# Softmax sums over pairs of tiles: half of a layer's exponentials are added in twos on VectorE before TensorE sums them, and every engine's order is written anew

## The chip, the cores and the metric

One core of a Trainium2 chip runs the whole program. The metric is the device time of one execution in microseconds. Three executions of the kernel before took 3888.88, 3893.77 and 3896.64 us; their median, 3893.77 us, is the time before. Another execution was recorded by the hardware profiler; its rows are the source of all durations below.

## What is computed

The reference is one transformer layer on 16 images of 512 x 512 pixels:

```
h = patches(x) @ W + b                      # 1024 tokens of 256 per image
q, k, v = split(layernorm(h) @ w_qkv)       # 8 heads of 32
k = sum over f of a_f*sin(f*k) + b_f*cos(f*k), f = 1..256   # elementwise
h = h + softmax(q @ k.T * 32**-0.5) @ v @ w_out + b_out
h = h + shared_mlp(layernorm(h)) + top-2 of 4 experts
```

For the change only the softmax matters. The kernel never subtracts a maximum. It forms E = exp(scale * scores) with the keys on the partitions, and then two products with E as the moving operand: E with the values, and E with a block of ones. The second gives the sum of the exponentials of each query, already spread over the 32 rows that the division needs.

## The kernel before

**Tiling.** An image has four pairs of heads, and a pair has two halves of its queries, so there are 16 * 4 * 2 = 128 attention steps (`att`). A step walks over eight tiles of 128 keys (`kc`). For each `kc`:

- `score` (L1233): two matmuls (token S) write a tile of 128 keys x 1024 columns (two heads of 512 queries) into PSUM. The tile is one of two buffers, `big0` and `big1`, of two banks each.
- `exponential` (L1249): one ScalarE activation (token F) reads that tile and writes `es`, a 128 x 1024 tile in SBUF, one of five.
- `weigh` (L1261): token W, two groups of four matmuls. Each group uses the TensorE array as four column tiles of 32 and adds to one half of the PSUM tile `av`: the first with 32 columns of `v` as weights, the second with `ones32`. fp32 matmuls are issued in two passes, so the profile counts eight instructions for a group.

After the eighth tile, `normalize` (L1288) takes the reciprocal of the sums and multiplies, on VectorE.

**The other work in the same stretch.** The key transform of the following heads runs beside the attention. GpSimd turns integer phases (`turn_waves`, token T), ScalarE takes sines (`sine`, token F), TensorE mixes them into a PSUM tile (`mix`, token M, the array as 64 x 32 tiles), VectorE multiplies (`times_fast`, token P), and TensorE sums (`add_up`, token R). The mix tiles use the same two buffers `big0` and `big1` as the scores, in strict turns: each fill of a big tile must wait for the reader of the fill two places before. Four chains of further work (digits 0 to 3: keys, queries, values, tokens, projection and networks) use two PSUM banks of their own, `side0` and `side1`.

**Who sets the order.** Nothing is ordered at run time. `ORDERS` (L76) holds, for each of the five engines, a string in which each character is the next piece of work on that engine. `run` (L552) reads the strings and records the instructions; each engine then executes its own in that order, waiting only for data and buffers. VectorE's characters are P (`prod`), K (`keys`), N (`norm`), D (`spread`, a shuffle of 128 x 1024) and the chains' digits. `lay` (L527) records for each big tile who reads it last; `USERS` (L65) names that reader, `prod` for M and `exp` for S. The next fill of the buffer depends on it.

A digit's work on TensorE can be issued in two forms: with the whole 128 x 128 array (L408), or as four column tiles of 32 (L411). `tiling_of` (L384) takes the form that fits the neighbours, because a change of the array's form costs TensorE time.

**Values.** `values` (L740) projects two tiles of 128 tokens into a side bank; ScalarE copies them into `v` and, for the last pair of heads, into `last`, from where GpSimd copies them later (`last_values`, L768).

Of the kernel before, what the change touches and what calls it, by code (L numbers as in the profile page):

```python
# [11 lines left out]
FP = mybir.dt.float32  # L12
# [6 lines left out]
P = 128  # L19
# [29 lines left out]
NES = 5  # L49
GS = 4  # L50
# [20 lines left out]
    DVE: {"P": "prod", "K": "keys", "N": "norm", "D": "spread"},  # L71
# [7 lines left out]
        "33333331311",  # L79
        "111111000000FFFFFFFFFFF0FF0F0FF0FFF3333F33FFFFFFFFFFFF3",  # L80
        "333311113333000011130000000003D0D30PD0PD03PDPDDD3333PP00330D",
        "1100100T0TTTTTTTTTTTTTTTT0",
        "XXXXXXXX10XWWAA0AAWWWWW00WWW00W0WWWWXWAWAXWXAWQWAXQWX",
# [3 lines left out]
        "00300300303",  # L87
        "3333F3FFFFFFFFFFFFFFFFFFFF",
        "P3DP33333DK",
        "T3TTT3TTTTT0TTTT3TTT3TTTT0TTTTT0TTTTTT0T",  # L90
        "0WWXSWWKWWKWWWXWA0WQA0AWWAWXWXWWW",
# [3 lines left out]
        "MM00RM00M0R0MM3R3033M3M3RM3M30R3MM3SSRS0SSWWSSWS30WMMWWWWMMRSSRSSWWSSWSSW3WWWMW0MMMRSSRS"  # L95
        "SWSWSSWSWWWW0WMMMRM0SSRSSWSWSSWSWWWMWMW0MRMSSSWSWSSWSSWRWWWWMMMMRSSSWSSWSWSSWWRWWW0M0MM0"
        "M0SSRWSSRWWSS3WS3SWWWW3MM31RMM1SSRSWSSWSWSSWWWWW3MM31MRSS0SMWWWS3SR3SS1SWWWWW0MMMRMS0SSR"
        "WSS1W1SS1W1S0WWWW1MMW1RM1S01SMWSS1SSW1SSWRW101WMMWWWR1MM1SSR1SSW1SSWWSS1W1MMWWWWMMRS0S1S"
        "R1SSW1W1SS1SWWW01WMMW1RWMM3SS1SS1SSWWW1SSWRWWWW301MM131SS0S1SSRWMMWWS0SSR310WMMWWWWR1SM1"
        "SMWW3SS1SSW3SSRWWWW1MMW3RMM1SS0SS1SSWWRSSW1WW3MMWWW3M13SSR1SSWMW1WS3SW31SSWR1WWW1MM01R1M"  # L100
        "M1SS0SSRWWSSW1SSW01WW1WMMW0RMM10SS1SSRW1WSSW1SSW1WW1MMWWSS3SS0SSRWWMMW1SSW0RWWW1MM1W3R1M"
        "M1SS3S1SSWWWSS1SRWW1WWW101",
        "FFFFFFFFFFFFFFFFFFFFFFFFFFFFFFFFFFFFFFFFFFFFFFFFFFFFFFFFFFFFFFFFFFFFFFFFFFFFFFFFFFFFFFFF"
        "FFFFFFFFFFFFFFFF0FFF0FFF0FF0FFFF3333F3F3FFFFFFFFFFFFFFFFFFFFFFFFFFFFFFFFFFFFFFF3333F3F3F"
        "FFFFFFFFFFFFFFFF11F1F1F1F1F1F2FFFFFF1FFF1FFFF1F2F1FFF1FF1FFF1FFFFFF1FFFFFF1FF1FFFFFFFFFF"
        "FFFFFFFF1111FFF1F1FF1FF21FFFFFF1FFFFF1FFF2FF1FF1FFF1FFFFFFFF10FFFF1FFFF0FFF1F0FFFFFFFF10"
        "FFFFFFF3F3F33F3FFF3FFFFFFFFFFFFFFFFFFFFFFFFFFFFF111FFF1FFF1FFFFF13333F31F32FFFF1FFFF1FFF"
        "1FFF1F21FFFFFF1FFF1FFFFFFF1FFFFFFF1FF1FFFFFFFFFFFFFFFFFFFFF1F11F1FFFF1FF1FFF1FFFFFF12FFF"
        "1FFFF1F2FF1FFFF1F",
        "PPD0003PPDD3DD000030PP0NPPNNDNDDDKNNPPPPNNDDDD030NPPNNNPPDDKD0DPNPNPNPND0DDDNNNPNPPPDDKD"  # L110
        "NDPPNNPPN3333DDDDN3NPNNP1PPDDK1D3N3NDPNNP331P333D0PD00DD11111N0P0P0PNPDNN000DDK1002PPD0N"
        "PDNN2NP0D2DDPPN1NPPNDND10KD1D11111PPPPNNDNND0D1D2PP0NNPP2NND2DK3DN3NNDPP31NDPPDDD3P3P333"
        "1NNPNN1PDD1DKDPP1NNNPP3D1ND10DD0111110P3PNNN3NP33333DPD1DKD2NPP0N0N0PP2D2N00D0DD000PPNN0"
        "PP1NND0DK1D1D1PPNN1111N3NDPP0DD0DPPN3N1NPPN2DDK32D2NNNDN",
        "TTTTTTTTTTTTTTTTTTTTTTTTTTTTTTTTTTTTTTTTTTTTTTTTTTTTTTTTTTTTT3TTTT3TTTTTTTTTTTTTTT0TTTTT"
        "3TTTTTT0TTT1T0TT3TT0TTTTTTTT022T2TT2TTTTTTTTTTTTTTTTTTTTT1TTTTTTTTTTTTT2222TTTTTTTTTTTTT"
        "TTTTTTTTTTT3TTTTT3TTTTTTT0TTTTTTT1TTTT0TT3TTT3TTTTTTTT2022T2TTT0TTTT0TTTTTTTTTTTTTTTT1TT"
        "TTTTTTTTTT2TTTTTT22T2TTT",
        "S0WKWWKWWQWWAWW0AXAWWA0WWWWSWWKQWW0WKWW0WWQWAAWAAWWWQWWWSWQKWWWKWWWAQAWWWXAAWWWWSWWXKWWW"
        "WWWKWWQAAW0AWAWWWQXW0XWWSW0KWKW0WWWQW0WAWAAAWWWWWWW0SWQKKWWWW10QWWWAWAXWA0WWAWWQWWSWKWKX"  # L120
        "WWWXQXWWWWQAWWAWWAAWW1WWSWKWXKWWWWWWAQXXQWAWWAAXWW0WWXWSWWKWKWW0WWQAWAA0W0WAWW0WWQW0WSK1"
        "WKWXWWWWW0QW0AAWWWWAAQXXWWWQWSKK",
    ),
    (
        11,
        "MM1MMR1RSS10SS1SSW1WW1SSW0WWWWMM1RMM3SS0SSWWRSS1SS3WWWWWW1MM310MM1SSRRSS1SSWWSSW3W3WMMWW"
        "3W31SSR1SSW1MMW1S3SWR3SSWW10W1WMMW1RMM1S0S1SSWWR1SS0SSWW1WWWW10MM10MM1SSRWSS1WWR1SS0SS1W"
        "WWWWMM1SSR0WSSWMMWW1SS31SSWRWWW13MM13MMR1SS1SSWWSS1SSWRW1WWWW101",
        "F1FFF1FF10FFFF1F1F0FFFFFF0FFFFFFFFFFF0FFFF3333F3FFFFFFFF3FFFFFFFFFFFFFFFFFFF1F1F1FF1FFFF"
        "1FF1FF331332F3F3FF2FF1FFFFF1FFFF1FFF1FF1FFF1FFF1FFFFF1FFFFFFFF1FF1FFFFFFFFFFFFFFFFFFFFFF"  # L130
        "1111F1F1FFFFF1FFFFFFFFFF12FFF1FFF12FFF1FFFFF1F",
        "PPPP1DDDD1NNPP1PNPND3D3333KDD1N1PNNPN10PP010D1DD11131DP3P3NN3N333N3DPP1D2DKD000P2PN2NPPN"
        "N0D00DD0D00NN0P1PNPPND0D1DKD10NPNNP1N111D1D0PP3DDNNNN3P1PP3PD22DD2KNNDNN",
        "TTTTTTTTTTTTTTTTT3TTTTTT0TTT3T0TTTTT1TTTTTTT3TTTT22TTTTT20TT2T3T0TTTTT0TTTTTTTTTTTTTTTTT"
        "T1TTTTTTTTTTTTTT22T2TTTT2TT",
# [39 lines left out]
def plain_path(ctx: ExitStack, tc: tile.TileContext, a: dict, out: bass.AP, verdict: bass.AP):  # L175
# [1073 lines left out]
    def exponential(att, kc):  # L1249
# [7 lines left out]
        if old >= 0:  # L1257
            deps.append(("av", *divmod(old, NT)))
# [887 lines left out]
```

## Time and profile before

| what | value | where |
|---|---|---|
| median of three runs | 3893.77 us | times |
| profiled execution's own time | 3891.19 us | times |
| its span, first to last instruction | 3889.6 us | page |
| TensorE (PE) busy | 3789.0 us, 97% | page, part 1 |
| ScalarE (ACT) busy | 3261.8 us, 84% | page, part 1 |
| GpSimd (POOL) busy | 3199.8 us, 82% | page, part 1 |
| VectorE (DVE) busy | 2530.3 us, 65% | page, part 1 |
| DMA engines, largest queue | 81.5% of 16 engines' span | page, part 3 |
| granted TensorE clock | 0.992 of full | times |

In the page, part 1 gives the busy time of each engine and its share of the span. Part 2 cuts the span in 40 slices of 97 us; a digit is the busy share in tenths. Part 5 has groups of equal instructions: line, engine, operation, output and inputs, sizes, count, then total busy time, mean duration in ns of one, and the engine's idle time just before them. Busy time of TensorE overlaps, since a matmul starts before the one in front has drained: four column tiles start 7 ns apart, and what they cost the engine is read from one group's start to the next one's, not from the mean.

### The profile page before, as it was taken

How to read it: one execution, taken by the hardware profiler on the slowest of the kernel's cores; microseconds unless marked ns; L12 is line 12 of the kernel's file. 1: busy time of each engine (PE TensorE's matmuls, PEld its weight loads, DVE VectorE, ACT ScalarE, POOL GpSimd, SP SyncE). 2: the span in 40 equal slices, each digit the busy share in tenths (PEclk: the TensorE clock that was granted, in tenths of full speed). 3: DMA queues.
4: the chain of work that ended last, by engine and by line, in shares of the span. 5: the costliest groups of instructions: out<-in, count | busy, mean ns of one | idle time of the engine just before them, and what ended most of it. 6: DMA issues, size and time to landing. Idle time of an engine off the chain costs nothing.

```text
span 3889.6 us, 104231 instructions
## 1 busy us (share of the span) xinstructions
PE 3789.0 (97%) x41057; PEld 1937.2 (50%) x41057; DVE 2530.3 (65%) x4075; ACT 3261.8 (84%) x3939; POOL 3199.8 (82%) x2328
## 2 busy tenths in 40 slices
PE   6899999999999999999999999999999999999998
PEld 4434454454545555455454545555455454544444
DVE  3756757667675766757667676766767667676652
ACT  1799888888888988888888888888888888888983
POOL 3989878788888888888888888888888888888860
PEclk8999999999999999999999999999999999999999
DMA  6998878879879888888979889788888889878760
GB/s 210 265 270 236 259 228 236 256 215 275 232 242 249 225 268 233 254 234 241 253 219 274 229 246 255 218 269 236 251 243 240 252 225 277 221 232 246 224 173 18
DMA packets 589668, 916.61 MB, mean 236 GB/s; under 512 B 60876, under 2 KB 179572, under 8 KB 589172
## 3 DMA queue, kind: packets, MB, share of 16 engines
q1 hardware_dynamic: 588036, 909.40, 81.5%
q8 instruction: 327, 5.36, 0.6%
q14 instruction: 169, 1.38, 0.1%
q10 hardware_dynamic: 1136, 0.47, 0.1%
HBM read 758.64 MB, written 150.99 MB: 234 GB/s over the span
## 4 chain that ended last, share of the span: by engine, by line
PE 79%; DMA 7%; ACT 6%; DVE 3%; issue 2%; POOL 2%; SPq 1%; ACTq 0%; POOLq 0%; DVEq 0%
PE av L1271 20%; PE sT L1238 11%; PE kan L1139 10%; PE red L1172 5%; DMA w<-ud 4%; PE tok L411 4%; PE tok L408 4%; PE e3p L408 3%; PE e1p L408 3%; PE e1p L411 2%; ACT w L1119 2%; PE proj L408 2%; PE k L408 2%; PE s1p L411 2%; PE lnT L417 1%
## 5 line engine op out<-in xcount | busy, mean ns | idle before, releaser
L1109 POOL TENSOR_TENSOR w<-w,lane 128x1024 int32<-128x1024 int32 x1024 | 1928.2, 1898 | 296.4 <-DMA w<-ud 186.4
L1253 ACT ACTIVATE es<-sT 128x1024 f32<-128x1024 f32 x1024 | 1014.1, 1024 | 339.2 <-PE sT L1238 309.2
L1109 POOL TENSOR_TENSOR f<-f,lane 128x1024 int32<-128x1024 int32 x512 | 972.0, 1898 | 152.0 <-DVE f L1094 89.5
L1119 ACT ACTIVATE w<-w 128x1024 f32<-128x1024 int32 x1024 | 1016.1, 1048 | 58.8 <-POOL w L1109 47.7
L1153 DVE TENSOR_TENSOR f<-kan,f 128x1024 f32<-128x1024 f32 x512 | 613.3, 1218 | 291.5 <-PE kan L1139 135.3
L1238 PE MATMUL sT<-q,k 128*128 128x512 f32 x2048 | 677.2, 446 | 21.4 <-ACT es L1253 7.4
L1094 DVE STREAM_SHUFFLE f<-src 128x1024 int32<-128x1024 int32 x512 | 686.4, 1369 | 0.7
L1271 PE MATMUL av<-es,v 128*32 128x256 f32 x8192 | 638.9, 384 | 5.9 <-ACT es L1253 5.5
L1271 PE MATMUL av<-es,ones 128*32 128x256 f32 x8192 | 630.0, 379 | 0.0
L1139 PE MATMUL kan<-w,coef 64*32 64x512 f32 x8192 | 525.3, 597 | 8.3 <-ACT w L1119 6.9
L1119 ACT ACTIVATE f<-f 128x1024 f32<-128x1024 int32 x512 | 514.9, 1046 | 4.6 <-POOL f L1109 4.6
L1238 PEld LDWEIGHTS sT<-q,k 128*128 128x128 f32 x2048 | 359.0, 189 | 258.0 <-issue 104.5
L1271 PEld LDWEIGHTS av<-es,v 128*32 128x32 f32 x8192 | 228.4, 109 | 348.9 <-issue 225.4
L1295 DVE RECIPROCAL rc<-av 128x256 f32<-128x256 f32 x128 | 224.6, 1755 | 265.1 <-PE av L1271 264.9
L1271 PEld LDWEIGHTS av<-es,ones 128*32 128x32 f32 x8192 | 266.4, 110 | 176.1 <-issue 0.5
L1139 PEld LDWEIGHTS kan<-w,coef 64*32 64x32 f32 x8192 | 129.9, 105 | 295.9 <-issue 129.3
L1172 PE MATMUL red<-f,pack 128*32 128x512 f32 x2048 | 272.7, 602 | 3.2 <-DVE f L1153 3.1
L411 PE MATMUL tok<-wt,x 128*32 128x256 f32 x3456 | 199.8, 379 | 3.2 <-DVE h L643 3.2
L1119 ACT ACT_TABLE_LOAD x128 | 164.2, 1283 | 21.9 <-DMA w<-ud 19.7
L408 PE MATMUL tok<-wt,x 128*128 128x256 f32 x672 | 161.4, 393 | 14.9 <-DMA x<-in_xT 11.2
L1391 ACT ACT_TABLE_LOAD x128 | 164.2, 1283 | 2.2
L605 ACT ACTIVATE hn<-h,less,rstd 128x256 f32<-128x256 f32 x256 | 138.2, 595 | 21.6 <-POOL less L597 21.1
(150 smaller groups left out, 4257.1 us busy)
## 6 DMA issues: line engine op xcount, KB each, us to landing
w<-ud SPq DMA_DIRECT2D x2048, 256.0 KB
q<-qd SPq DMA_DIRECT2D x512, 128.0 KB
k<-kd SPq DMA_DIRECT2D x256, 256.0 KB
x<-in_xT SPq DMA_DIRECT2D x128, 384.0 KB
ud<-u SPq DMA_DIRECT2D x64, 512.0 KB
ud<-ui SPq DMA_DIRECT2D x64, 512.0 KB
src<-ud SPq DMA_DIRECT2D x512, 64.0 KB
qd<-qhi SPq DMA_DIRECT2D x64, 256.0 KB
```

Source lines behind the costliest of these rows:

```text
L408: nc.tensor.matmul(out=out, lhsT=lhsT, rhs=rhs, start=start, stop=stop)
L411: nc.tensor.matmul(out=out[ts(i, 32)], lhsT=lhsT[:, ts(i, 32)], rhs=rhs, start=start, stop=stop)
L1094: nc.vector.stream_shuffle(w, sources[g // 8].rearrange("p r n -> p (r n)"), [4 * (g % 8) + i // 8 for i in range(32)],)
L1109: nc.gpsimd.tensor_tensor(w, w, f.to_broadcast([P, N]), ALU.mult)
L1119: nc.scalar.activation(x, w, AF.Sin, scale=TURN * 2.0**-32)
L1139: nc.tensor.matmul(out=ps[ds(64 * j + 32 * blk, 32), ts(r, 512)], lhsT=coef[ts(r, 64)].rearrange("p e f j -> p (e f j)"), rhs=w[ts(r, 64), ...
L1153: nc.vector.tensor_mul(w, kan.pop(g), w)
L1172: nc.tensor.matmul(out=rows_of_pair[p][ts(2 * i + r, 32), :], lhsT=pack[:, ds(PACK0 - 16 * (k % 2) - 2 * (k // 2), 32)], rhs=prod[:, ts(r, ...
L1238: nc.tensor.matmul(out=ps[:, ts(s, 512)], lhsT=k4[kc // 4][:, s, ts(kc % 4, P)], rhs=q4[:, s, :], start=True, stop=True,)
L1253: nc.scalar.activation(es, scores.pop(kc), AF.Exp, scale=SCALE)
L1271: nc.tensor.matmul(out=acc[0][ts(i, HD), ts(half, 256)], lhsT=ones32 if half else v[:, kc, p % NPAIR, ts(i % 2, HD)], rhs=es[:, ds(512 * ( ...
L1295: nc.vector.reciprocal(rc[0], acc[0][:, 256:512])
```

## The change

In each attention step the key tiles 1 and 5 are put in `SUMMED`. Such a tile and the one in front of it form a pair, so two of the four pairs of a step, (0,1) and (4,5), are treated in a new way; (2,3) and (6,7) stay as they were.

- The first tile of a pair goes through `exponential` as before, but is multiplied with the values only, not with the ones.
- The second tile's exponentials are written back into its own score tile in PSUM. A new VectorE operation, `pair_sum` (token U), adds them to the first tile's and writes the sum into SBUF. The sum is multiplied with the values and with the ones.
- So that the result stays the same, the values of the first tile are stored as a difference: E0*V0 + E1*V1 = E0*(V0 - V1) + (E0 + E1)*V1. `values` forms V0 - V1 on VectorE out of the side bank, after ScalarE has copied V1.
- The big buffer of a summed tile is freed by `pair_sum`, no longer by the exponential. The SBUF tile of the pair's first tile is freed by its own matmuls and by the sum.
- The five order strings are replaced throughout.

The core of the diff, with the order strings left out:

```diff
+SUMMED = (1, 5)
...
-    DVE: {"P": "prod", "K": "keys", "N": "norm", "D": "spread"},
+    DVE: {"U": "sum", "P": "prod", "K": "keys", "N": "norm", "D": "spread"},
...
-            user = USERS.get(kind)
+            user = "sum" if kind == "S" and key[2] in SUMMED else USERS.get(kind)
...
-            yield ACT, 0.56
-            src = ps.rearrange("p t (i s d) -> p t i s d", s=2, d=HD)
-            for s in range(2):
-                nc.scalar.copy(
-                    v[:, ds(t0, 2), 0 : NPAIR - 1, ds(HD * s, HD)],
-                    src[:, :, 0 : NPAIR - 1, s, :],
-                )
-            nc.scalar.copy(last[:, ds(t0, 2), :, :], src[:, :, NPAIR - 1, :, :])
+            held = chains[now["chain"]]["bank"]
+            yield ACT, 0.31
+            chains[now["chain"]]["bank"] = held
+            homes = (
+                (v[:, :, 0 : NPAIR - 1, :].rearrange("p t i d -> p t (i d)"), slice(0, 192)),
+                (last, slice(192, 256)),
+            )
+            if t0 + 1 not in SUMMED:
+                for home, part in homes:
+                    nc.scalar.copy(home[:, ds(t0, 2), :], ps[:, :, part])
+                continue
+            for home, part in homes:
+                nc.scalar.copy(home[:, t0 + 1, :], ps[:, 1, part])
+            yield DVE, 0.42
+            for home, part in homes:
+                nc.vector.tensor_sub(home[:, t0, :], ps[:, 0, part], home[:, t0 + 1, :])
...
-            es = exps[kc] = esp.tile([P, 1024], FP, tag=f"es{(att * NT + kc) % NES}", name="es")
-            nc.scalar.activation(es, scores.pop(kc), AF.Exp, scale=SCALE)
...
+            ps = es = scores[kc]
+            if kc not in SUMMED:
+                es = exps[kc] = esp.tile([P, 1024], FP, tag=f"es{(att * NT + kc) % NES}", name="es")
+            nc.scalar.activation(es, ps, AF.Exp, scale=SCALE)
...
+    def tile_free(att, kc):
         old = att * NT + kc - NES
+        if old < 0:
+            return []
+        deps = [("av", *divmod(old, NT))]
+        return [*deps, ("sum", old // NT, old % NT + 1)] if old % NT + 1 in SUMMED else deps
+
+    def pair_sum(att, kc):
+        def action():
+            both = exps[kc] = esp.tile([P, 1024], FP, tag=f"es{(att * NT + kc) % NES}", name="both")
+            nc.vector.tensor_add(both, scores[kc], exps[kc - 1])
+
+        deps = [("exp", att, kc - 1), ("exp", att, kc)] + tile_free(att, kc)
+        put(DVE, "sum", 1.14, deps, ("sum", att, kc), action)
...
-            for half in range(2):
+            for half in range(1 if kc + 1 in SUMMED else 2):
...
-        deps = [("exp", att, kc)]
+        deps = [("sum" if kc in SUMMED else "exp", att, kc)]
...
-        put(PE, "W", 0.86, deps, ("av", att, kc), action)
+        put(PE, "W", 0.43 if kc + 1 in SUMMED else 0.86, deps, ("av", att, kc), action)
```

`last_values` makes one copy in place of two.

## The prediction

> **What bounds the kernel now.** First the totals and the slices.
>
> ```profile
> PE 3789.0 (97%) x41057; PEld 1937.2 (50%) x41057; DVE 2530.3 (65%) x4075; ACT 3261.8 (84%) x3939; POOL 3199.8 (82%) x2328
> ...
> PE   6899999999999999999999999999999999999998
> ```
>
> TensorE has no slice under nine tenths but the first two and the last. The busy times by stage (columns: stretch, its length, busy time of PE, weight loads, DVE, ACT, POOL, then clock, DMA share, GB/s) say how tight that is:
>
> ```profile
> 0.00:30.00 30.00, 18.78 (x80) 16.32 (x81) 4.90 (x17) 3.23 (x5) 4.07 (x26) 1.00 0.74 207
> ...
> 100.00:150.00 50.00, 37.72 (x348) 17.14 (x348) 34.63 (x54) 33.60 (x50) 45.61 (x34) 0.87 0.94 259
> ...
> 200.00:300.00 100.00, 92.01 (x1029) 35.55 (x1020) 60.42 (x82) 90.71 (x97) 89.88 (x49) 0.98 0.96 262
> ...
> 1000.00:2000.00 1000.00, 992.40 (x11068) 517.40 (x11057) 669.19 (x1072) 870.18 (x1058) 852.06 (x611) 1.00 0.86 243
> 2000.00:3000.00 1000.00, 994.60 (x11169) 514.98 (x11168) 681.55 (x1107) 873.11 (x1057) 857.97 (x626) 1.00 0.85 243
> ```
>
> From 400 us on TensorE idles 5 to 8 us in a thousand; ACT, POOL and DMA stand at 85 to 87%. In the first 300 us DMA (up to 0.96) sets the pace. So a TensorE microsecond is a microsecond of the kernel over some 95% of the attention, until waits appear. They hardly exist now (engine, line waited for: total us, times, longest):
>
> ```profile
> PE sT L1238 <- ACT es L1253: 7.4, 13, 1.9
> ...
> PE sT L1238 <- DVE f L1153: 5.2, 10, 1.0
> ```
>
> These two, with kan<-DVE f 0.9 and kan<-ACT es 0.2, are the waits for a big PSUM buffer: 13.7 us in all. It is the resource that the change strains.
>
> **What is removed.** Counted in both instruction orders, the matmuls with ones go from 4096 to 3072, so 256 groups of four are gone: 128 steps x 2 pairs. The change does what it says. A group's cost is read from starts in the timeline, since busy times overlap (start, busy us):
>
> ```profile
> 1904.33 0.61 PE L1271 MATMUL av<-es,ones 128*32 128x256 f32 x8
> 1904.76 0.61 PE L1271 MATMUL av<-es,v 128*32 128x256 f32 x8
> 1905.19 0.61 PE L1271 MATMUL av<-es,ones 128*32 128x256 f32 x8
> ```
>
> The starts are 0.43 us apart: 256 x 0.43 = **110 us** off TensorE. (Part 5's 630.0 us over 1024 groups would give 0.615 us and 157 us; it counts each drain.)
>
> **What the new order adds on TensorE.** Each change of the array's form costs. I took the time from the first matmul of one group to the first of the next, less streaming, median per kind of change, and counted the changes before and after (for whole to 128x32, whose median 0.28 holds waits for scores, I take 0.235, the lower quartile):
>
> - whole to 128x32: 389 to 478, at 0.235: +20.9 us
> - 128x32 to whole: 308 to 428, at 0.144: +17.3
> - 64x32 to 128x32: 135 to 189, at 0.171: +9.2
> - 128x32 to 64x32: 215 to 238, at 0.138: +3.2
> - whole to 64x32: 69 to 96, at 0.104: +2.8
> - 64x32 to whole: 149 to 145, at 0.171: -0.7
>
> Together 309 more changes, **+53 us** (46 to 57 with the least and the median value of the first kind). The Trainium skill (TensorEngine Tiling, Tiling Modes) says that changing the mode, not just the tile, drains the engine: a rule against this change, which halves the gain by cutting the stream finer. It states no price. TensorE: Matmul & The Clock Gate (What happens when you issue a matmul) puts a drain at about 128 cycles, at 2.4 GHz 53 ns; as an estimate that makes 309 x 0.053 = 16 us and a net gain of 94. The rows show two to four times that, and I go by them: net 110 - 53 = 57 us, of which 95%, **54 us**, falls where TensorE is the bound.
>
> **What VectorE gets.** The 256 sums read PSUM and SBUF and write SBUF, as the product does:
>
> ```profile
> L1253 ACT ACTIVATE es<-sT 128x1024 f32<-128x1024 f32 x1024 | 1014.1, 1024 | 339.2 <-PE sT L1238 309.2
> ...
> L1153 DVE TENSOR_TENSOR f<-kan,f 128x1024 f32<-128x1024 f32 x512 | 613.3, 1218 | 291.5 <-PE kan L1139 135.3
> ```
>
> 256 x 1.22 = 312 us, and 32 differences of 192 and of 64 columns at about 0.35 and 0.22 us (scaled from the 256-column addition, 0.42, and the 512-column one, 0.69) are 18: busy 2860 us, 75% of the new span. That much hides beside TensorE; what doesn't is its latency.
>
> **What ScalarE gets.** 256 exponentials write PSUM in place of SBUF, a form that the trace doesn't have. ScalarE: Activation LUTs (Step-by-step) calls PSUM the faster port for its output. The nearest row is the same activation into SBUF, 1.024 us. VectorE: DVE Perf Modes (The TRN2 errata) has the other side, reading PSUM rather than SBUF, at 52 cycles of 1.2 GHz less, 0.043 us; carried over to the write, as an estimate, it makes 0.98. The widest row of its size is the sine, 1.048. I take 1.02; from -11 to +6 us on an engine that isn't the bound, under 0.05 us on each sum's path. The value copies get cheaper (64 x (2 x 0.32 + 0.29) = 60 us to some 43, by row lengths). Both hide under TensorE's 97%; without that cover they'd be worth -17 us. The side bank is held longer for 32 of 64 value tiles, by ScalarE's wake-up and 0.6 us of VectorE. GpSimd's 16 copies for 32 save nothing that waits. No DMA is added; the queue orders are other permutations of the same transfers.
>
> **The wait that is added.** A big buffer with a summed tile is held by score, exponential and sum, and the fill two places on, score or mix, waits, with everything behind it in TensorE's single queue. In the trace the exponential ends at the soonest 1.24 us after the scores have streamed (median 1.6), the product 1.55 after the mix; the next fill follows within 0.05. A summed tile thus needs 1.24 + 0.06 + 1.22 + 0.05 = 2.57 us at least. Against that I set the streamed TensorE work, with the changes' prices, between a big tile and the next fill of its buffer, and carried each shortfall forward:
>
> - before, at these least delays: 11 short fills, 5 us, nearly all before 400 us. The measured 13.7 us answers to delays about 0.4 us longer.
> - after: of 256 summed tiles a quarter have under 2.94 us of cover (median 3.37) and 39 fall short; so do 28 after plain exponentials and 19 after products. After 400 us the shortfall is 13 us at the least delays, 33 with 0.3 us more, 42 with 0.4, 76 with 0.6.
>
> More work is packed between scores, but less than the hold grows. 138 of the 256 sums stand right behind a spread (1.37 us) and 43 behind the step that closes a normalization, so VectorE will often be some tenths late: I take **+30 us**, between 13 and 76. Behind a late sum waits its W as well, but it has 3.65 us of cover in nine of ten cases.
>
> **The sum.** Span 3889.6 - 54 + 30 = 3865.6. The median of the runs lies 4.2 us above that span (2.6 above the profiled execution's own 3891.19): 3870. The first 300 us are ordered anew as well and may give or take some 10 us; ScalarE's relief shortens exponential waits a little, for which I take 4 off. Predicted: **3866 us**, -0.7%.
>
> **Rivals.**
>
> *The sums hide* (chance 0.15): the order meets VectorE in time, the wait stays near 13 us or the start gains. 3894 - 54 + 8 to 13 = about 3848. For it: VectorE has 1360 us idle. Against: 39 sums lack cover even at the least delay.
>
> *The big buffers become the bound* (0.26, slower): in place, the PSUM buffers of summed tiles. If sums come 0.6 us over the least delay, the shortfall is 76 us against 54 gained: 3894 + 22 = 3916. It decides from about 0.48 us of mean lateness, where the shortfall reaches 54. For it: a spread or reciprocal (1.75 us) in front of a sum costs more than that if it starts late, and VectorE goes from 65 to 75%. Against: before, exponentials came 0.36 late in the median and cost 13.7 us.
>
> *Another engine is the bound already* (0.09, no change): the wave transfers hold GpSimd (186.4 us of its waits are on them), DMA is at 0.85, and the chain that ended last has 7% DMA. Then the freed time turns into TensorE idle and the median is about 3892. Against: ACT, POOL and DMA each have 13% to spare, and 1.4% is asked.
>
> **How the numbers follow.** The forecast as told has 0.50; with the hidden sums 0.65 faster by over 0.2%. 0.2%, 8 us, is about what a measurement of this kernel tells from no change. No change: 0.09. Slower: 0.26. The range leaves out the best half of the first rival and the worst of the second: 3838 to 3916; the forecast's own is 3848 to 3885.
>
> **What would show it.** Right: L1271's ones rows at three quarters of their count; PE busy near 3720; waits of sT and kan on VectorE's sum, 10 to 50 us; the sum near 1.22 us. Wrong: the in-place exponential over 1.1 us; changes of form that cost less than their medians; TensorE idling on `w` or `f` in the middle slices.

## The result: 0.75% slower, not 0.7% faster

The changed kernel takes 3920.73 us (median of 13 runs, 3902.68 to 3949.72), the kernel before 3892.89 us beside it (13 runs, 3886.11 to 3899.86). The ratio is 1.0075, with a 95% interval of 1.0058 to 1.0092: 28 us more, where 28 us less was predicted, and 5 us beyond the range. The profiled execution took 3926.66 us with a span of 3925.0.

The totals and the slices of the kernel after:

```profile
PE 3768.8 (96%) x39573; PEld 1833.0 (47%) x39573; DVE 2814.9 (72%) x4395; ACT 3257.3 (83%) x3875; POOL 3194.9 (81%) x2312
...
PE   7899999999999999999999999999999999999998
```

TensorE issues 1484 matmuls fewer and is busy for only 20 us less. The slices look as before. Busy time by stage (the same columns as in the prediction: stretch, length, PE, weight loads, DVE, ACT, POOL, clock, DMA share, GB/s):

```profile
1000.00:2000.00 1000.00, 981.97 (x10626) 484.81 (x10618) 733.94 (x1151) 862.57 (x1032) 843.12 (x604) 1.00 0.84 241
2000.00:3000.00 1000.00, 981.17 (x10735) 485.34 (x10734) 748.49 (x1174) 862.95 (x1029) 849.16 (x607) 1.00 0.84 242
```

Where 5 to 8 us in a thousand were idle on TensorE, 18 to 19 are now. ScalarE, GpSimd and the DMAs are each a point or so less busy, so none of them has simply become full. The groups that the change touches, after (line, engine, operation, tiles, count, then busy time, mean ns of one, and idle time just before them with its releaser):

```profile
L1277 ACT ACTIVATE es<-sT 128x1024 f32<-128x1024 f32 x768 | 770.3, 1021 | 307.4 <-PE sT L1260 288.8
...
L1175 DVE TENSOR_TENSOR f<-kan,f 128x1024 f32<-128x1024 f32 x512 | 609.5, 1214 | 259.2 <-ACT f L1141 137.4
...
L1292 DVE TENSOR_TENSOR both<-sT,es 128x1024 f32<-128x1024 f32 x256 | 312.6, 1221 | 194.5 <-ACT sT L1277 192.4
L1307 PE MATMUL av<-es,ones 128*32 128x256 f32 x4096 | 316.9, 380 | 0.0
L1277 ACT ACTIVATE sT<-sT 128x1024 f32<-128x1024 f32 x256 | 260.5, 1018 | 56.1 <-ACT es L1277 20.1
```

The durations are close to those of the prediction: the sum takes 1.221 us (1.22 forecast), the exponential into PSUM 1.018 (1.02). The ones are 4096 matmuls into `av` from `es` and 2048 from the sums, three quarters of the 8192 before. What TensorE waits for, after (line waited for, total us, times, longest):

```profile
PE sT L1260 <- DVE both L1292: 34.8, 47, 2.2
PE sT L1260 <- DVE f L1175: 18.1, 33, 3.0
PE kan L1161 <- ACT w L1141: 12.5, 11, 2.6
PE sT L1260 <- ACT es L1277: 12.5, 17, 2.4
```

Waits of a fill on the sum, 34.8 us, are in the forecast's 10 to 50. Three of the four signs for a right forecast thus came true: the count of ones, the length of the sum and the waits on it. The fourth did not: TensorE was to be busy for some 3720 us and is busy for 3768.8. And one of the signs against it shows faintly: between 400 and 3600 us TensorE waits 12 us on products (`f`) and 5 on sines (`w`), where it waited 4 and 1 before. The chain that ended last changed most of all. Its shares before, then after:

```profile
PE 79%; DMA 7%; ACT 6%; DVE 3%; issue 2%; POOL 2%; SPq 1%; ACTq 0%; POOLq 0%; DVEq 0%
```

```profile
PE 58%; ACT 13%; DMA 11%; DVE 8%; issue 4%; SPq 2%; POOL 2%; ACTq 0%; DVEq 0%; POOLq 0%
```

ScalarE, the DMAs, VectorE and GpSimd had 18% of it together; after, these four have 34%.

### The profile page after: what moved, and what is told of

Its sections match the earlier page's. It is cut to its first block, busy times and chain, and to the rows that moved or that the text cites. A ratio compares the mean times of both kernels' runs of the same rounds, so it can differ in the third digit from the quotient of the medians.

```text
span 3925.0 us, 101002 instructions
## 1 busy us (share of the span) xinstructions
PE 3768.8 (96%) x39573; PEld 1833.0 (47%) x39573; DVE 2814.9 (72%) x4395; ACT 3257.3 (83%) x3875; POOL 3194.9 (81%) x2312
## 4 chain that ended last, share of the span: by engine, by line
PE 58%; ACT 13%; DMA 11%; DVE 8%; issue 4%; SPq 2%; POOL 2%; ACTq 0%; DVEq 0%; POOLq 0%
PE av L1307 13%; PE sT L1260 10%; PE kan L1161 7%; DMA w<-ud 6%; ACT w L1141 5%; PE red L1194 4%; PE tok L428 3%; ACT f L1141 3%; PE e1p L425 2%; DVE f L1116 2%; PE tok L425 2%; PE e3p L425 2%; DVE f L1175 2%; PE e1p L428 2%; DVE both L1292 2%
## 5 line engine op out<-in xcount | busy, mean ns | idle before, releaser
L1277 ACT ACTIVATE es<-sT 128x1024 f32<-128x1024 f32 x768 | 770.3, 1021 | 307.4 <-PE sT L1260 288.8
L1260 PE MATMUL sT<-q,k 128*128 128x512 f32 x2048 | 724.4, 456 | 84.6 <-DVE both L1292 34.8
L1161 PE MATMUL kan<-w,coef 64*32 64x512 f32 x8192 | 543.5, 600 | 15.1 <-ACT w L1141 12.5
L1260 PEld LDWEIGHTS sT<-q,k 128*128 128x128 f32 x2048 | 343.9, 189 | 418.4 <-issue 123.5
L1307 PE MATMUL av<-es,v 128*32 128x256 f32 x6144 | 484.9, 386 | 1.4 <-ACT es L1277 1.1
L1292 DVE TENSOR_TENSOR both<-sT,es 128x1024 f32<-128x1024 f32 x256 | 312.6, 1221 | 194.5 <-ACT sT L1277 192.4
L1307 PE MATMUL av<-es,ones 128*32 128x256 f32 x4096 | 316.9, 380 | 0.0
L1277 ACT ACTIVATE sT<-sT 128x1024 f32<-128x1024 f32 x256 | 260.5, 1018 | 56.1 <-ACT es L1277 20.1
L1307 PEld LDWEIGHTS av<-es,v 128*32 128x32 f32 x6144 | 164.4, 109 | 302.8 <-issue 230.4
L1307 PEld LDWEIGHTS av<-es,ones 128*32 128x32 f32 x4096 | 134.0, 110 | 88.9 <-issue 1.3
```

Of the source, the lines that this page charges most:

```text
L1161: nc.tensor.matmul(out=ps[ds(64 * j + 32 * blk, 32), ts(r, 512)], lhsT=coef[ts(r, 64)].rearrange("p e f j -> p (e f j)"), rhs=w[ts(r, 64), ...
L1260: nc.tensor.matmul(out=ps[:, ts(s, 512)], lhsT=k4[kc // 4][:, s, ts(kc % 4, P)], rhs=q4[:, s, :], start=True, stop=True,)
L1277: nc.scalar.activation(es, ps, AF.Exp, scale=SCALE)
L1292: nc.vector.tensor_add(both, scores[kc], exps[kc - 1])
L1307: nc.tensor.matmul(out=acc[0][ts(i, HD), ts(half, 256)], lhsT=ones32 if half else v[:, kc, p % NPAIR, ts(i % 2, HD)], rhs=es[:, ds(512 * ( ...
```

## The experiments

Each was timed beside the kernel before on the same chip; differences below are of medians. By the intervals a median is good to some 4 to 13 us. Runs of different rounds come from different chips; the kernel before beside them differs by up to 4.5 us. All times in one place:

| run | median, us | before beside it | ratio (95%) |
|---|---|---|---|
| no_ones | 3842.02 | 3891.23 | 0.9881 (0.9864 to 0.9897) |
| short_sum | 3888.61 | 3891.23 | 0.9989 (0.9976 to 1.0002) |
| exp_in_sbuf | 4016.67 | 3891.23 | 1.0323 (1.0305 to 1.0341) |
| new_orders_no_sums | 3944.48 | 3891.23 | 1.0129 (1.0108 to 1.0150) |
| bank_released | 3919.56 | 3891.82 | 1.0073 (1.0045 to 1.0101) |
| old_orders_1_5 | 4186.92 | 3891.82 | 1.0761 (1.0728 to 1.0793) |
| old_orders_7 | 3891.66 | 3891.82 | 0.9994 (0.9980 to 1.0008) |
| old_orders_6_7 | 3931.73 | 3891.82 | 1.0105 (1.0079 to 1.0131) |
| twice_ones | 3973.53 | 3889.63 | 1.0217 (1.0194 to 1.0240) |
| half_exp | 3874.97 | 3889.63 | 0.9962 (0.9951 to 0.9973) |
| no_ones_half_exp | 3809.75 | 3889.63 | 0.9797 (0.9777 to 0.9818) |
| no_ones_half_turn | 3800.31 | 3889.63 | 0.9778 (0.9755 to 0.9800) |
| half_turn | 3867.43 | 3892.84 | 0.9926 (0.9904 to 0.9947) |
| no_ones_half_both | 3757.08 | 3892.84 | 0.9655 (0.9633 to 0.9677) |
| after_half_turn | 3875.41 | 3892.84 | 0.9953 (0.9937 to 0.9968) |
| old_orders_6_7_short | 3877.04 | 3892.84 | 0.9951 (0.9931 to 0.9971) |
| half_both | 3849.53 | 3894.15 | 0.9885 (0.9858 to 0.9912) |
| new_orders_no_ones | 3887.44 | 3894.15 | 0.9983 (0.9973 to 0.9993) |

### First: each part alone

**no_ones**: the kernel before, without the ones of tiles 0 and 4. It is the gain of the change with nothing paid for it.

```diff
-            for half in range(2):
+            for half in range(1 if kc in (0, 4) else 2):
```

> The kernel before with its own orders; the matmuls of key tiles 0 and 4 with the ones are left out and nothing takes their place, so the softmax sums lack two tiles of eight. It measures the gain by itself: 256 groups of four matmuls at 0.43 us, 110 us of TensorE. If TensorE is the bound of nearly all of the attention, the time falls by 95 to 110 us, to 3785 to 3800. If another engine or the transfers stand close behind it, the time falls by less than 60 us, to over 3835.

It gains 49 us, not the 104 that the prediction's step makes of 110. The totals and two stages of this run:

```profile
PE 3708.7 (97%) x39009; PEld 1865.4 (49%) x39009; DVE 2526.4 (66%) x4075; ACT 3260.0 (85%) x3939; POOL 3195.6 (83%) x2328
```

```profile
1000.00:2000.00 1000.00, 987.65 (x10656) 508.73 (x10655) 678.23 (x1096) 881.36 (x1069) 864.82 (x620) 1.00 0.86 246
2000.00:3000.00 1000.00, 991.03 (x10716) 500.71 (x10701) 692.23 (x1118) 883.76 (x1072) 869.28 (x631) 1.00 0.87 249
```

In each thousand us some 430 matmuls fewer are issued, and TensorE is still busy for 98.8 to 99.1% of it. Its busy share can hardly tell the two kernels apart, and so had not shown before how tight TensorE really was.

**new_orders_no_sums**: the strings of after without their 256 U, every tile with its ones, values copied and not subtracted (VectorE copies what it would have subtracted). It is the price of the order alone.

```diff
-SUMMED = (1, 5)
+SUMMED = ()
+APART = (1, 5)
...
-                nc.vector.tensor_sub(home[:, t0, :], ps[:, 0, part], home[:, t0 + 1, :])
+                nc.vector.tensor_copy(home[:, t0, :], ps[:, 0, part])
```

> The changed kernel's orders without sums: every tile is multiplied with values and ones as before the change, the sums are taken out of VectorE's order, and V0 is copied by VectorE, not subtracted. TensorE has the work of the kernel before in the new order. It measures the price of the new order: 309 more changes of form at 40 to 53 us, so 3935 to 3950 if the order costs no more than these. If the order also brings waits of its own that have nothing to do with the sums, 3960 to 4000. If the counted changes of form are cheap in truth, under 3920.

It loses 53 us, which is the prediction's price for 309 more changes of the array's form. (The run prices the whole order; how much of it are changes of form is counted below.)

**short_sum**: the kernel after, but a sum adds 32 of 1024 columns, and its tile's exponential goes straight to SBUF. The sum's length is gone and its hold of the buffer is short (the next fill still waits for the short sum); the order and the matmuls stay.

```diff
-            ps = es = scores[kc]
-            if kc not in SUMMED:
-                es = exps[kc] = esp.tile([P, 1024], FP, tag=f"es{(att * NT + kc) % NES}", name="es")
+            ps = scores[kc]
+            es = exps[kc] = esp.tile([P, 1024], FP, tag=f"es{(att * NT + kc) % NES}", name="es")
...
-            nc.vector.tensor_add(both, scores[kc], exps[kc - 1])
+            few = slice(0, 32)
+            nc.vector.tensor_add(exps[kc][:, few], scores[kc][:, few], exps[kc - 1][:, few])
```

> The changed kernel with its orders, but VectorE's sum touches 32 columns of 1024, and the second tile's exponentials go straight to SBUF; the product then uses the second tile's exponentials nearly alone, so the softmax lacks the first tile's share in the sums. The big PSUM buffer is held for the exponential and a short VectorE operation. If the lateness and length of the sums at the big buffers (and the products that they delay) are what cost the forecast gain, some 60 to 85 us come back: 3835 to 3860. If the new orders by themselves are the cause (changes of form, other waits), the time stays within 15 us of 3921.

It is 32 us faster than the kernel after (3920.73) and level with the kernel before. The first lines of TensorE's waits in it:

```profile
PE sT L1260 <- DVE f L1175: 18.7, 39, 3.2
PE sT L1260 <- ACT es L1276: 14.3, 19, 1.9
PE kan L1161 <- ACT w L1141: 11.7, 10, 2.9
PE lnT L434 <- ACT hn L622: 11.7, 9, 5.6
```

Fills waited 34.8 us on the sum in the kernel after; on the short sum it is 3.1 us in six waits, the others are much as they were, and the time fell by about as much. So the sums cost some 30 us, as was forecast for the hold, though the run takes away length and hold together and can't tell which of them counts. It came out between the two outcomes that were named for it: even without that cost the kernel is only level with the one before, so the gain must be missing somewhere else.

**exp_in_sbuf**: the kernel after, with the exponentials of tiles 1 and 5 in SBUF and the sum in place there. The big buffer is free after the exponential, and the sum keeps its length.

```diff
-            both = exps[kc] = esp.tile([P, 1024], FP, tag=f"es{(att * NT + kc) % NES}", name="both")
-            nc.vector.tensor_add(both, scores[kc], exps[kc - 1])
+            nc.vector.tensor_add(exps[kc], exps[kc], exps[kc - 1])
```

> The changed kernel with its orders and full sums, but the exponentials of tiles 1 and 5 are written to SBUF and summed there in place, so the big PSUM buffer is free after the exponential, as before the change. VectorE has the same sums in the same places of its queue, with both inputs in SBUF. If the hold of the buffer is the cause, its waits (about 50 us at the fills behind summed tiles) go: 3860 to 3880. If VectorE as a queue is the cause (the sum at its head waits for ScalarE and delays the products behind it), the time stays at 3905 to 3930. If the two SBUF inputs slow GpSimd's phases, it could also be longer than 3930.

It is 96 us slower than the kernel after. Its groups say why; the first row is that of the kernel after, for comparison:

```profile
L1131 POOL TENSOR_TENSOR w<-w,lane 128x1024 int32<-128x1024 int32 x1024 | 1926.3, 1894 | 297.8 <-DMA w<-ud 210.3
```

```profile
L1131 POOL TENSOR_TENSOR w<-w,lane 128x1024 int32<-128x1024 int32 x1024 | 2012.5, 1979 | 195.9 <-DMA w<-ud 122.6
...
L1131 POOL TENSOR_TENSOR f<-f,lane 128x1024 int32<-128x1024 int32 x512 | 1032.2, 2016 | 103.3 <-DVE f L1116 85.6
...
L1290 DVE TENSOR_TENSOR es<-es 128x1024 f32<-128x1024 f32 x256 | 443.9, 1734 | 186.8 <-ACT es L1276 186.4
```

The sum takes 1.734 us in place of 1.221, and GpSimd's turns 1.98 to 2.02 in place of 1.89: GpSimd is busy for 3400.0 us, VectorE for 2946.1 (3194.9 and 2814.9 after). The Trainium skill (SBUF — State Buffer, Who interferes with whom) says that a VectorE instruction with two SBUF inputs contends with a GpSimd instruction that reads SBUF, and calls their shared port pair an exclusive lock. The trace agrees: the 166 sums that start inside a turn take 2.01 us in the mean and up to 2.94, the other 90 take 1.23, and in the kernel after no sum takes over 1.25. So this run did not separate the hold from the sum's length, as it was meant to; but it was the first sign that GpSimd's chain stands right behind TensorE's: GpSimd grew by 205 us and the kernel by 96, and GpSimd's share of the chain that ended last went from 2% to 14%. It isn't proof, since VectorE grew as well, by 131 us, and TensorE's `weigh` waits 32 us for the longer sums, where it waited for none.

### Second: the buffers' hold, under the order of before

The theory that I held at this point was that the gain goes into the big buffers, and that pairs placed where the old order leaves cover would keep it.

**bank_released**: the kernel after, with the side bank held until VectorE has subtracted only where there is a difference to form.

```diff
-            chains[now["chain"]]["bank"] = held
+            if t0 + 1 in SUMMED:
+                chains[now["chain"]]["bank"] = held
```

> The changed kernel with its orders; the side bank of a value tile is taken to be free for other chains as soon as ScalarE has copied it, where no difference is formed (in the changed kernel it stays reserved until the chain's next step, after the last value tile for as long as an attention step lasts). If the chains waiting for the one other bank cost TensorE time, the time falls by 15 us or more, to under 3905. If the cause lies at the big buffers, it stays within 8 us of 3921.

3919.56 us, as the kernel after: the bank plays no part that a run good to 11 us can show.

**old_orders_1_5**, **old_orders_7**, **old_orders_6_7**: the code of after under the strings of before, where VectorE's sums and subtractions stand in no string and are put in as soon as their inputs are there. The first keeps the pairs (0,1) and (4,5); the second has the single pair (6,7); the third pairs (4,6) and (5,7), whose fills two places on are far away in the old order. The third against the code of after, without the values' part:

```diff
-SUMMED = (1, 5)
+SUMMED = (6, 7)
...
-            nc.vector.tensor_add(both, scores[kc], exps[kc - 1])
+            nc.vector.tensor_add(both, scores[kc], exps[kc - 2])
...
-            for half in range(1 if kc + 1 in SUMMED else 2):
+            for half in range(1 if kc + 2 in SUMMED else 2):
```

> The sums of the changed kernel, on tiles 1 and 5, under the orders of the kernel before; VectorE's sums and differences, which these orders don't have, are put in as soon as they can start. No change of form is added; TensorE has 110 us less work. Under the old order a summed tile has a median of 2.5 us of TensorE work until the next fill of its buffer, under the 2.57 us that it needs at least: the same tally as in the prediction gives 65 us of waits at the least delay, and 220 us if sums come as late as measured after the change (0.85 us in the mean). So with the hold as the cause: 3860 at the best, 3920 to 4010 likely. If the sums' place at the big buffers doesn't matter and the new order is at fault, 3790 to 3810.

> One pair only, tiles 6 and 7, under the orders of the kernel before; sums put in as soon as they can start. 128 groups of ones are gone, 55 us of TensorE. Behind tiles 6 and 7 the old order has a median of 8 to 9 us of other TensorE work before the next fill of their buffers, so the hold is covered and the tally gives no wait for the sums. With the hold as the cause of the loss: 3840 to 3850. If VectorE's load and queue are the cause, with half as many sums: no gain, 3880 to 3900.

> Two pairs again, but (4,6) and (5,7), so that both sums stand on tiles 6 and 7, where the old order has cover; orders of the kernel before, sums put in as soon as they can start. The same 256 groups of ones are gone as in the change, VectorE has the same 256 sums, and the same values are stored as differences (V4 less V6, V5 less V7). The tally gives 2 to 5 us of waits for sums. With the hold as the cause of the loss, nearly all of the 110 us shows: 3795 to 3820, faster than both kernels. If VectorE's load is the cause whatever the tile, 3880 or more.

The first is 295 us slower than before, more than any count made it. One line of TensorE's waits in it carries nearly all of that:

```profile
PE sT L1270 <- DVE both L1302: 294.0, 216, 6.8
```

In the old order scores often stand back to back, and there the hold is ruinous. Keeping clear of that is what the new order's more frequent changes of form seem to pay for. A part is the clock: it was granted at 0.978 in this run and at 0.992 before, which on some 3780 us of TensorE work makes, as an estimate, 50 us. Why a single sum is up to 6.8 us late there I did not follow up.

The other two decide against the theory. One pair in a well-covered place gains nothing (3891.66 beside 3891.82), and two pairs lose 40 us, where the theory let them gain 70 to 100. The first lines of TensorE's waits in old_orders_6_7:

```profile
PE wT L418 <- POOL bands L863: 27.4, 12, 3.9
PE sT L1270 <- ACT es L1287: 15.9, 32, 3.5
PE lnT L418 <- ACT hn L631: 13.0, 12, 4.0
PE kan L1171 <- ACT w L1151: 12.4, 13, 1.8
```

No fill that waits for a sum is among them; further down seven fills do, for 5 us in all. TensorE waits for GpSimd's `bands`, a step that doesn't appear among the waits of TensorE before, and for ScalarE. With the hold nearly out of the way, the kernel is slower all the same.

### Third and fourth: who takes the other half

A new theory was needed for the half of 110 us that TensorE no longer works and the kernel still takes. Its claim: ScalarE and GpSimd, at 84% and 82%, form a chain (turn, sine, mix, product, and the exponentials between) that is nearly as long as TensorE's stream, though neither is full. If so, ones must be worth more once these two are relieved, and adding ones must cost more than leaving them out gains.

**twice_ones**: the kernel before, with the ones of tiles 0 and 4 issued twice.

```diff
-            for half in range(2):
+            for half in (0, 1, 1) if kc in (0, 4) else (0, 1):
```

> The kernel before with its own orders; the matmuls of tiles 0 and 4 with the ones are issued twice, so these tiles count twice in the softmax sums. TensorE gets the 110 us that the run without them lost. If TensorE is the bound and what stands behind it is only a little faster, adding costs in full, 100 to 110 us (3990 to 4002), while taking away gave 49. If TensorE's time has been worth half all along, since waits take up the rest in either direction, it costs 45 to 60 us (3937 to 3952).

110 us more of TensorE cost 84 us; 110 us less gained 49. One slope to both sides would have made them alike. (Neither of the outcomes named for it, 100 to 110 or 45 to 60, came.)

**half_exp** and **no_ones_half_exp**: exponentials of 512 of 1024 columns, which the products read twice (1024 x 0.43 us off ScalarE), with and without the ones of tiles 0 and 4. **half_turn** and **no_ones_half_turn**: GpSimd turns 512 of 1024 columns (1306 us off GpSimd), in the same two ways. The two edits:

```diff
-            nc.scalar.activation(es, scores.pop(kc), AF.Exp, scale=SCALE)
+            nc.scalar.activation(
+                es[:, 0:512], scores.pop(kc)[:, 0:512], AF.Exp, scale=SCALE
+            )
...
-                        rhs=es[:, ds(512 * (i % 2) + 256 * (i // 2), 256)],
+                        rhs=es[:, ts(i % 2, 256)],
```

```diff
-            nc.gpsimd.tensor_tensor(w, w, f.to_broadcast([P, N]), ALU.mult)
+            half = w[:, 0:512]
+            nc.gpsimd.tensor_tensor(half, half, f.to_broadcast([P, 512]), ALU.mult)
```

> The kernel before with its own orders; each exponential covers 512 of 1024 columns, and the products read these columns twice, so half of the queries get the other half's weights. ScalarE loses some 0.43 us on each of 1024 exponentials, 440 us of 3262, and big buffers come free that much sooner; TensorE's work is the same. If TensorE's own work is nearly all of the time (97% busy), it falls by 30 us or less: 3860 to 3890. If waits for ScalarE are a good part of it, by more than 50: under 3840.

> The same short exponentials, and the ones of tiles 0 and 4 left out as well. The difference to the run with short exponentials alone is the gain of the 256 groups when ScalarE isn't near. If ScalarE, as the reader of the scores and the sender of the sines, is what took half of the gain, 90 to 110 us come out between the two runs. If it is something else (GpSimd's chain, VectorE, the transfers), 40 to 60 again.

> The kernel before with its own orders; GpSimd turns 512 of 1024 columns of each wave tile, so half of the phases aren't turned. It is the control for the same with the ones left out (3800). If GpSimd limits only once TensorE is shorter, the time stays within 20 us of 3890, and the ones are worth 70 to 90 us with GpSimd relieved. If GpSimd's lateness is already in the time, it falls by 35 to 45, and the ones are worth 45 to 55 as before: then GpSimd isn't what took the other half.

> The ones of tiles 0 and 4 left out, and GpSimd turns 512 of 1024 columns of each wave tile, so half of the phases of the key transform are not turned. GpSimd loses some 1400 of 3200 us. If GpSimd's chain took half of the gain of the missing ones, the time falls from 3842 to 3785 to 3805. If ScalarE or the big buffers did, it stays within 15 us of 3842.

Relieved alone, ScalarE gives 15 us and GpSimd 25: neither bounds the kernel before. But leaving the ones out now takes it from 3874.97 to 3809.75, 65 us, and from 3867.43 to 3800.31, 67 us. Each is some 17 us over the 49 of before, and good to 9 to 12 us; half_turn and no_ones_half_turn come from different rounds, and set against the kernels before beside them the 67 are 64. Alone, either would be a hint at most, and no_ones_half_exp and half_turn fell between the outcomes named for them.

**half_both** and **no_ones_half_both** relieve both at once, with the two edits together.

> The kernel before with its own orders, exponentials over 512 columns and turns over 512 columns, ones kept. If the two reliefs only add (25 and 15 us), 3850 to 3858, and the ones are then worth 93 to 101 us to the run without them (3757): ScalarE and GpSimd together took the missing half. If the reliefs help each other without any change on TensorE, under 3830, the ones are worth less than 73 and something else takes a part.

> The ones of tiles 0 and 4 left out, exponentials over 512 columns and turns over 512 columns. If ScalarE and GpSimd each took a part of the gain, and what is left of the waits is at the start and in other places, 3775 to 3790. If the two reliefs act on one and the same chain, no more than the half turns alone: 3795 to 3805.

From 3849.53 to 3757.08: the ones are worth 92 us (91 set against the kernels before beside them), give or take 14. That is what the theory asks, and most of the 104 that the prediction reckoned with (no_ones_half_both came out faster than either outcome named for it). VectorE's work and the transfers were left as they were, and the transfers run at a share of 0.87 to 0.90 in the middle of the faster kernel (0.85 to 0.86 before): so neither is needed to explain the missing half. What the runs don't separate is load from delay, since a shorter exponential also frees its big buffer sooner. The shares of the chain that ended last, half_both:

```profile
PE 91%; DMA 3%; DVE 2%; ACT 1%; issue 1%; SPq 1%; POOL 0%; DVEq 0%; ACTq 0%; POOLq 0%
```

This is how the chain looks when TensorE nearly alone bounds a kernel. The `PE 79%` of before, with ScalarE, VectorE, GpSimd and the DMAs in it, was not that.

**after_half_turn**: the kernel after with the half turns.

> The changed kernel with its orders and sums, GpSimd's turns over 512 columns. If GpSimd's chain is what stands behind TensorE in the new order as well, 30 to 45 us come back: 3876 to 3891. If in the new order the late sums at the big buffers and VectorE's queue limit, less than 15: over 3906.

It gains 45 us on the kernel after, where the kernel before gains 25 from the same edit. So GpSimd's chain seems to weigh more in the kernel after (the two gains are each good to 9 us or so), and with it relieved the change loses only 8 us (3875.41 against half_turn's 3867.43), good to some 10, not 28.

**old_orders_6_7_short**: old_orders_6_7 with sums of 32 columns and exponentials straight into SBUF.

> Pairs (4,6) and (5,7) under the orders of the kernel before as in the earlier run, but each sum touches 32 of 1024 columns and the second tile's exponentials go straight to SBUF, so the softmax nearly lacks the first tiles in its sums. The big buffers wait for the short VectorE operation still. If the length of the sums on VectorE made that run 90 us slower than the one without ones, the time is 3842 to 3865. If it was the places in VectorE's order (a sum at the head waits for its exponential and the products wait behind it), 3900 or more.

3877.04 against 3931.73: there the full sums cost 55 us more than the short ones, though fills hardly wait for them. VectorE's time is not free even where TensorE doesn't wait for its result: what GpSimd gets from VectorE comes later. GpSimd's turns behind VectorE's spread (`f<-f`) show it, in old_orders_6_7 and then with the short sums:

```profile
L1141 POOL TENSOR_TENSOR f<-f,lane 128x1024 int32<-128x1024 int32 x512 | 971.3, 1897 | 217.1 <-DVE f L1126 129.7
```

```profile
L1141 POOL TENSOR_TENSOR f<-f,lane 128x1024 int32<-128x1024 int32 x512 | 971.5, 1897 | 150.1 <-DVE f L1126 73.6
```

The idle time ahead of them falls from 217.1 to 150.1 us, that on VectorE from 129.7 to 73.6, and TensorE's waits for `bands` fall from 27.4 to 0.8.

The 55 us are not the sums' length alone. As these sums stand in no string, their places follow from the length that the program reckons with, and some 60 of VectorE's operations stand elsewhere in the run with short sums; also, the granted clock is 0.992 in its profile and was 0.988. And the short sums are still 35 us slower than no sums at all (3842.02, no_ones): the run came between the two outcomes named for it, and that rest stays unexplained.

### Fifth: the gain and the sums under the new order

**new_orders_no_ones**: new_orders_no_sums, with the ones of tiles 0 and 4 left out.

```diff
-            for half in range(1 if kc + 1 in SUMMED else 2):
+            for half in range(1 if kc + 1 in APART else 2):
```

> The changed kernel's orders without sums (3944 us), and the ones of tiles 0 and 4 left out with nothing in their place, so the softmax sums lack two tiles of eight. If the groups are worth half in this order as well, 50 to 60 us: 3885 to 3895, and the sums then cost the 25 to 35 us that are left to 3921. If the new order hides ScalarE and GpSimd better, 75 or more: under 3870, and the sums cost over 50.

3887.44 us. Now the way from before to after can be walked in three steps, each a measured difference: the new order +53 (3891.23 to 3944.48), the ones -57 (3944.48 to 3887.44, timed beside kernels before that differ by 3 us), the sums +33 (3887.44 to 3920.73). That they add up to +29, beside the 28 measured, is no test, since each step starts where the one in front ends; what the run tells is that the ones are worth 57 us in the new order too, and how the rest splits. It also confirms short_sum, whose 3888.61 us lie within 4 us of it, with or without the kernels before taken off: in this order short sums cost next to nothing.

The same can be seen inside the traces. From the starts of TensorE's groups I took, for each group, the time to the next group's start, less the streaming of its columns, less the change of form at the lower quartile of its kind; what is left is waiting. How much of it is called streaming depends on the rate taken for a column, by some 65 us, and waiting then moves by some 20 the other way and the changes of form by the rest; the differences between kernels stay. In us, one profiled execution each:

| kernel | streaming | changes of form | waiting | span |
|---|---|---|---|---|
| before | 3472 | 228 | 171 | 3889.6 |
| no_ones | 3362 | 228 | 224 | 3833.6 |
| half_both | 3472 | 228 | 116 | 3835.2 |
| no_ones_half_both | 3362 | 228 | 141 | 3750.9 |
| new_orders_no_sums | 3472 | 268 | 182 | 3944.2 |
| new_orders_no_ones | 3362 | 268 | 232 | 3884.6 |
| after | 3362 | 268 | 272 | 3925.0 |

(The rest of a span, 19 to 23 us, is before the first group and behind the last.) In the kernel before, some 150 to 171 us were waiting already, where the busy time shows 100 us of idleness. Without the ones the streaming falls by 109 and the waiting rises by 53, with the two engines relieved by 25 only. In the kernel after, of 101 us more of waiting than before, 49 are fills behind sums and some 30 are more fills behind products.

## Why the prediction was wrong

**The removal, 110 us off TensorE: right.** The streaming fell by 109.

**Its worth: this is the step that failed.** The prediction reads: "So a TensorE microsecond is a microsecond of the kernel over some 95% of the attention, until waits appear." It made 104 us of 110, before the order's price. Measured: 49 in the old order, 57 in the new one, about half. It rested on TensorE's idle time of 5 to 8 us in a thousand. ("From 400 us on" is a misreading: that holds from 1000 to 3000 us; its own windows have 13 in a thousand from 400 to 1000 and 11 from 3000 to 3600.) But busy time of pipelined matmuls covers drains and short waits: it stayed at 98.8% and more in the middle when 110 us were taken away. The Trainium skill has this rule (Perfetto Trace Analysis, Identifying the Most-Contended Engine): matmul busy time is a bad measure of how close TensorE is to its peak, and it names the share of weight loads among the better ones. The first half is borne out. The second would not have helped: that share was 50% before, where the ones were worth 49 us, and 50% in half_both, where they were worth 92.

**The rival that was dismissed.** "Against: ACT, POOL and DMA each have 13% to spare, and 1.4% is asked." An engine's idle share is no reserve when its work comes in a dependent chain that hands over between engines: the idle time was waits, of ScalarE on TensorE's scores (309 us), of GpSimd on wave transfers (186) and of the engines on each other. With 0.43 us off each exponential and 0.85 off each turn, ones are worth 92 us; with one of the two, 65 and 67. The rival had the mechanism half right and its size wrong: no single engine is the bound, and TensorE's time isn't worth nothing, it is worth half. I had given it 0.09.

**The order's price, +53: right.** The run gave +53. The rule of the Trainium skill on changing the tiling mode (TensorEngine Tiling, Tiling Modes) was right against this change; the estimate of 16 us that the prediction made for it from the 128-cycle drain (TensorE: Matmul & The Clock Gate, What happens when you issue a matmul) was too low, and the rows of the trace were the better source. In the count, 40 of it are changes of form at their cheapest and 11 are more waiting, so that the agreement to the microsecond is luck.

**The hold of the big buffers, +30: right in size, in part by luck.** The sums cost 33 us (new_orders_no_ones to after), and 32 come back with short sums. They end some 3.2 to 3.4 us after the scores in the mean and 3.0 to 3.1 in the median (by how the end of the scores is taken), where the least was 2.5 to 2.6. That is a mean lateness of some 0.75 us, more than the 0.48 at which the prediction let the hold eat the whole gain; its tally makes 76 us of 0.6. So it took too little lateness and priced it too high. Nor was it VectorE that was late in the main, as forecast behind a spread or a reciprocal: a sum starts 0.03 us after its exponential has ended in the median, 0.28 in the mean. VectorE waits there, and what stands behind the sum in its queue waits too:

```profile
DVE both L1292 <- ACT sT L1277: 192.4, 146, 4.8
```

At 146 of 256 sums VectorE sat idle until ScalarE was through.

**What was costed at nothing.** The exponential into PSUM is free (1.018 us). The relief of ScalarE's value copies, for which I took 4 us off, shows nowhere: fills waited 12.5 us on exponentials, 7.4 before. Up to 400 us the kernel after waits some 12 us longer by the same count, about the 10 that were allowed for the start; new_orders_no_sums, with the same order, doesn't (82 us for 85 before), so it isn't the order.

So the sum should have been 3894 - 57 + 53 + 33: 3923. Of the rivals, "the big buffers become the bound" named 3916, near in number, but not by the mechanism: its shortfall of 76 us against a gain of 54 never came, since the sums cost 33 and half of the gain was missing.

## What to carry to other kernels

Before an engine's saved microsecond is booked as a microsecond, look at the chain that ended last: a bound engine had 91% of it here, and with 79% a saving was worth about half. It is a sign and no scale: half_exp has 82%, where the saving was worth 65, and so has twice_ones, where it was worth 84. Where other engines stand above 80% and feed each other, leave the work out and measure what the saving is worth before paying for it with a new order. And work given to an engine with idle time is not free: sums with hardly a fill behind them still cost up to 55 us, in part through what VectorE then handed on late.

## What the runs showed that I had not expected

- Two SBUF inputs on VectorE cost more than the PSUM hold that they avoid: 1.734 us for 1.221 a sum, and 0.09 to 0.12 us on each of GpSimd's 1536 turns in the mean; the kernel is 96 us slower with them.
- The cost of TensorE work was not symmetric: 110 us less gained 49, 110 more cost 84.
- An exponential into PSUM was only 3 ns faster than one into SBUF in the same kernel (1018 and 1021), 16 in old_orders_6_7 (1008 and 1024). The estimate of 0.98 that the prediction made from a page was too low.

What stays open: what the sums cost by their hold of the buffer and what by their time on VectorE; how the missing half of the ones splits between ScalarE and GpSimd (65 and 67 us are the same within the uncertainty, and together they give more than each), which of the handovers between them is the longest, and where the last dozen us lie between the 92 measured and the 104 reckoned with, if they are more than the uncertainty. No version that still computes the whole softmax was measurably faster than the kernel before.
